# Softmax weights of 26 more attention steps turned on VectorE and through DRAM, with a larger arena and later key jobs

## The chip, the core and the metric

The kernel runs on one core of a Trainium2 chip. Its time is the device time of one execution in microseconds, and the number that counts is the median of several executions. The core's engines are called as the profile calls them: PE (TensorE, matmuls), PEld (its weight loads), DVE (VectorE), ACT (ScalarE), POOL (GpSimd) and SP, whose queue issues nearly all DMAs here. Each engine works through its own instructions in the order in which the program holds them.

## What is computed

Four transformer blocks work one after the other on x of shape 8 x 112 x 256 (8 batches, 112 rows, 256 columns), in float32. All cross attention reads the same context of 8 x 375 x 192. Cut to what matters:

```python
# block 0 and block 1: 16 heads of 64
x = x + attention(ln(x), ln(x)) @ Wo1 + bo1          # self attention
x = x + attention(ln(x), context) @ Wo2 + bo2        # cross attention
a, gate = split(ln(x) @ Wp + bp); x = x + (a * gelu(gate)) @ Wf + bf
# block 2: cross attention alone, 16 heads of 64
x = x + attention(ln(x), context) @ Wo + bo
# block 3: 16 heads of 16, causal and padding masks
x = x + masked_self_attention(ln(x)) @ proj_w + proj_b
x = x + masked_attention(ln(x), context) @ out_w + out_b
x = x + gelu(ln(x) @ mlp1_w + mlp1_b) @ mlp2_w + mlp2_b
# attention: softmax over the keys of q k^T, times v
```

## The kernel before, in words

**Stages and steps.** The code numbers ten stages: 0 self attention, 1 cross attention and 2 feed-forward of block 0; 3, 4 and 5 the same of block 1; 6 the cross attention of block 2; 7 the self attention, 8 the cross attention and 9 the feed-forward of block 3. An attention stage is cut into steps (st, b, g): batch b and a group g of its heads. A cross step of stages 1, 4 and 6 has 4 heads, 4 steps to a batch; a step of stage 7 has 8 heads, 2 steps to a batch. The order of all steps is written out (`order`, `after`, L1271 and on): stage 7's steps are woven into stage 6 and stage 8, two at a time; (7,0) to (7,4) stand between and behind the steps of batches 4 to 7 of stage 6.

**A step** (`add_step`, L963) has these parts. S (`emit_s`) multiplies q by k into PSUM (L1055), 112 rows of queries by 375 or 112 keys, and emits the softmax: for heads of 64 the row maxima on DVE (L1006), the exponentials with their sums on ACT (L1012), the reciprocals on DVE (L1017) and the division on POOL (L1019); for heads of 16 mask and minimum on DVE (L992) and the exponentials on ACT (L1000), half of these in a part E of its own (`emit_late`), while the division comes later, on the product, in parts R and N. The weights of a head are then 112 queries x 375 (or 112) keys, with queries on the partitions. The product with v needs keys on the partitions, so the weights must be transposed. There are two ways:

- *On PE.* Part T (`emit_t`) transposes each head's weights in pieces of 128 keys by a matmul with the identity (L1085) into PSUM, four to a bank, and a copy on ACT or DVE brings each bank of 448 columns to SBUF (`evac`, L354 and L362, or L1092 and L1095 for heads of 16). PV (`emit_pv`, L1118) then multiplies by v.
- *Turned.* q is laid out with each 28 queries in a quarter of 32 partitions (so S gives 128 rows, of which 112 count), POOL clears the gaps (L718) and the padding (L982), and DVE transposes blocks of 32 x 32 (`flip`, L1028, STREAM_TRANSPOSE at L1033, two to a step). The 32 x 32 blocks are then in the wrong quarters: four DMAs write them to a DRAM buffer (`send`, L1039, 192 KB each) and one DMA reads them back in order (`fetch`, L961, 768 KB). PV takes them from there. `w_tile` and `d_tile` are two buffers each, so the fetch of a turned step waits for the PV of the turned step two before it. A turned step's S is emitted up to LEAD = 4 steps ahead of its PV (`lead`, L1546), others 2 steps. `turn_until` (L949) emits the DVE transposes of a step late, normally behind the softmax of the next S.

`TURN` (L1280) chooses: stages 1 and 4 are turned from (0,2) through batch 6, stage 6 from (0,2) through batch 3. That is 66 steps; stages 0, 3, 7, 8 and the second half of stage 6 transpose on PE.

**Planner.** PE's order is written by a planner at build time (`Plan`, L86). Projections, norms and feed-forward are items with a cost, a due step and what they need; the main loop (from L1556) emits S, T and PV of the steps in order and fills in items between them. q, k and v of coming steps lie in one SBUF arena of `ARENA` columns, and an item waits until the arena has room; an item that makes them isn't taken more than `ahead` steps before it is due (L269). Key and value jobs (`add_key_jobs`, `add_value_jobs`) are opened, with their first half emitted, by `open_jobs` (L184, called at L1614).

Of the kernel before, what the change touches and what calls it, by code (L numbers as in the profile page):

```python
# [17 lines left out]
S, DC = 375, 192  # L18
# [10 lines left out]
TURNED = (1, 4, 6)  # L29
# [56 lines left out]
class Plan:  # L86
# [4 lines left out]
    def __init__(self, rings, arena, size):  # L91
# [5 lines left out]
        self.now, self.step, self.ahead = 0.0, 0, 7  # L97
# [207 lines left out]
def kernel(ctx: ExitStack, tc: tile.TileContext, a: dict, out: bass.AP):  # L305
# [3 lines left out]
    ARENA = 9900  # L309
# [123 lines left out]
    cmask = const.tile([T, B, T], BF16, name="cmask")  # L433
    rb = const.tile([T, H, 16], F32, name="rb")
# [118 lines left out]
    def add_masks():  # L553
# [4 lines left out]
        def load():  # L558
            m8 = wpool.tile([T, B * (T + S)], U8, tag="w", name="m8")
            nc.sync.dma_start(m8[:, : B * T], a["mask_BxS_bf0"].rearrange("b t -> (b t)").partition_broadcast(T))  # L560
            nc.sync.dma_start(m8[:, B * T :], a["mask_BxS2_bf0"].rearrange("b s -> (b s)").partition_broadcast(T))
            got[src] = m8

        def self_mask():
            nc.gpsimd.tensor_scalar_mul(cmask.rearrange("p b t -> p (b t)"), got[src][:, : B * T], NEG)
            nc.gpsimd.affine_select(
                cmask, cmask, pattern=[[0, B], [-1, T]], compare_op=ALU.is_ge, fill=NEG, base=0,
                channel_multiplier=1,
            )
# [10 lines left out]
        for b in range(B):  # L580

            def ctx_mask(b=b):
                c = B * T + b * S
                nc.gpsimd.tensor_scalar_mul(got[key][:, b, :], got[src][:, c : c + S], NEG)
# [111 lines left out]
    def add_pair_projection(st, ring, j, w, us, deadline, scale=None):  # L696
# [3 lines left out]
        for u in range(us):  # L700
            key = (ring, st, j, u)

            def fn(u=u, key=key):
# [10 lines left out]
                if ring == "q" and st in TURNED:  # L714
                    kinds = [TURN(st, 2 * j + e, u) for e in range(2)]
# [23 lines left out]
    def add_last_projection(st, ring, j, w, wv, deadline, qb, kb=None):  # L739
# [5 lines left out]
        def fn():  # L745
# [8 lines left out]
            for e, key in enumerate(keys):  # L754
                t = place(key)
                for m in range(2):
                    src = ps[:, m * 2 * T : (m + 1) * 2 * T]
                    if ring == "q":
# [180 lines left out]
    def w_tile(s):  # L939
        return stage[:, (turned[s] % 2) * 1536 : (turned[s] % 2 + 1) * 1536]  # L940

    def d_tile(s):
        at = (2 + turned[s] % 2) * 1536
        return stage[:, at : at + 1536].rearrange("p (i x) -> p i x", i=NQ)

    emptied = [0]
    turns = deque()
# [15 lines left out]
    def add_step(st, b, blocks, dh, nk, qs, ks, qap, kap, vtile, mask, opos, ochunk, last=False, pair=None, turn=False):  # L963
# [9 lines left out]
        heads = [h for blk in blocks for h in blk]  # L973
        cell, late, slot = {}, [], {}

        def softmax(bi, blk, ps):
# [9 lines left out]
            if dh == 16:  # L986
# [3 lines left out]
                for n, h in enumerate(blk):  # L990
# [13 lines left out]
                    late.append(exp)  # L1004
                return pr
# [22 lines left out]
        def flip(bi, blk, whole):  # L1028
            w = whole[:, :]
            src = bass.AP(w.tensor, w.offset, [list(w.ap[0]), [nk, len(blk)], [P, nch], [32, NQ], [1, 32]])  # L1030
            dst = w_tile(s).rearrange("p (j h c t) -> p j h c t", j=NQ, h=4, t=32)
# [4 lines left out]
        def send():  # L1036
            dram = bounce.tile([NQ, 32, NQ, 384], F32, tag="b", name="b")
            for i in range(NQ):
                nc.sync.dma_start(  # L1039
                    dram[:, :, i, :].rearrange("j k x -> k j x"),  # L1040
                    w_tile(s)[32 * i : 32 * i + 32].rearrange("p (j x) -> p j x", j=NQ),
# [60 lines left out]
        def emit_pv():  # L1102
# [3 lines left out]
            if turn:  # L1106
                d = d_tile(s).rearrange("p i (h c t) -> p i h c t", h=4, t=32)
# [545 lines left out]
```

## Time and profile before

| What | Value |
|---|---|
| median of 3 executions | 1614.74 us (1613.98 to 1617.81) |
| the profiled execution | 1610.65 us, of which the span of its instructions is 1608.7 us |
| granted TensorE clock, mean | 0.994 |
| PE transposes of weights, L1085 | 1128 (384 of 112 x 112; 496 and 248 of the pieces of stages 1, 4, 6 and 8) |
| DVE transposes, L1033 | 132, busy 123.9 us |
| sends and fetches | 264 of 192 KB and 66 of 768 KB |
| DMA in all | 143.25 MB, 89 GB/s over the span |

The profile is one execution. Its page gives busy time per engine, the span in 40 slices, and a chain that ended last; further views group instructions by line and shape, list them in order of time (the timeline), sum them by stretch (the windows), and say who waited for whom. In the timeline a row gives start, duration, engine, line, what is written from what, a count when equal instructions were merged, and in brackets the idle time before and what ended it. A matmul of float32 values shows as two records, a transpose as one. Records of PE overlap, since matmuls are pipelined: what one costs PE is the distance between starts, not its duration.

In time, stage 1 lies at about 170 to 440 us, stage 4 at 670 to 945, stage 6 at 1040 to 1380 with its second half and (7,0) to (7,4) from 1190 on, and stage 8 with the rest of stage 7 at 1380 to 1575.

### The profile page before, as it was taken

How to read it: one execution, taken by the hardware profiler on the slowest of the kernel's cores; microseconds unless marked ns; L12 is line 12 of the kernel's file. 1: busy time of each engine (PE TensorE's matmuls, PEld its weight loads, DVE VectorE, ACT ScalarE, POOL GpSimd, SP SyncE). 2: the span in 40 equal slices, each digit the busy share in tenths (PEclk: the TensorE clock that was granted, in tenths of full speed). 3: DMA queues.
4: the chain of work that ended last, by engine and by line, in shares of the span. 5: the costliest groups of instructions: out<-in, count | busy, mean ns of one | idle time of the engine just before them, and what ended most of it. 6: DMA issues, size and time to landing. Idle time of an engine off the chain costs nothing.

```text
span 1608.7 us, 28898 instructions
## 1 busy us (share of the span) xinstructions
PE 1564.2 (97%) x10980; PEld 1069.2 (66%) x10980; DVE 842.4 (52%) x1996; ACT 743.9 (46%) x2396; POOL 538.7 (33%) x667
## 2 busy tenths in 40 slices
PE   9999999999999999998999989999999999999999
PEld 8778656565657878665666555665667666766667
DVE  3554565566522344455656532355555555678762
ACT  3453444434421444543444342134445555787772
POOL 1323344344402313334434330343433237212210
PEclk9999999999999999999999999999999999999999
DMA  6020165676601001035666721125650001000000
GB/s 179 9 70 23 51 190 182 192 211 177 191 30 53 20 5 53 28 101 158 194 196 201 207 68 30 38 56 167 192 163 21 1 1 42 31 2 2 2 1 24
DMA packets 74130, 143.25 MB, mean 89 GB/s; under 512 B 6807, under 2 KB 60695, under 8 KB 73991
## 3 DMA queue, kind: packets, MB, share of 16 engines
q1 hardware_dynamic: 73751, 141.23, 29.4%
q8 instruction: 86, 1.41, 0.4%
q14 instruction: 53, 0.43, 0.1%
q10 hardware_dynamic: 240, 0.17, 0.0%
HBM read 87.79 MB, written 52.82 MB: 87 GB/s over the span
## 4 chain that ended last, share of the span: by engine, by line
PE 77%; DVE 7%; ACT 6%; POOL 4%; DMA 3%; issue 2%; SPq 0%; DVEq 0%; ACTq 0%; POOLq 0%
PE mm L674 12%; PE mm L708 10%; PE s L1055 8%; PE mm L1118 8%; PE mm L815 6%; PE mm L1350 6%; PE mm L849 5%; PE mm L1085 5%; PE mm L824 4%; PE mm L774 4%; PE mm L858 3%; ACT pr L1012 3%; DVE stage L1033 2%; POOL pr L1019 2%; DVE nm L1006 2%
## 5 line engine op out<-in xcount | busy, mean ns | idle before, releaser
L1019 POOL TENSOR_TENSOR pr<-pr,rinv 128x750 f32<-128x750 f32 (+2 forms) x224 | 327.0, 1473 | 425.7 <-DVE rinv L1017 405.7
L1012 ACT ACTIVATE pr<-s,nm 128x375 f32<-128x375 f32 (+2 forms) x640 | 302.1, 489 | 244.2 <-DVE nm L1006 208.4
L1006 DVE TENSOR_REDUCE nm<-s 128x2 f32<-128x750 f32 (+2 forms) x224 | 206.4, 952 | 43.7 <-PE s L1055 41.7
L1055 PE MATMUL s<-arena 64*112 64x112 f32 (+4 forms) x1792 | 215.1, 397 | 6.5 <-ACT pr L1012 6.4
L362 DVE COPY arena<-mm 128x375 f32<-128x375 f32 (+6 forms) x198 | 114.9, 590 | 186.6 <-PE mm L858 74.1
L354 ACT COPY arena<-mm 128x375 f32<-128x375 f32 (+5 forms) x182 | 91.8, 509 | 232.8 <-PE mm L858 104.6
L1118 PEld LDWEIGHTS mm<-stage,arena 128*64 128x64 f32 (+5 forms) x3840 | 161.8, 130 | 42.0 <-issue 16.3
L1118 PE MATMUL mm<-stage,arena 128*64 128x112 f32 (+5 forms) x3840 | 180.4, 263 | 4.0 <-DMA stage<-b 2.9
L1055 PEld LDWEIGHTS s<-arena 64*112 64x112 f32 (+2 forms) x1792 | 116.9, 177 | 86.5 <-issue 29.9
L1085 PEld LDWEIGHTS mm<-ident,pr 112*128 112x128 f32 (+2 forms) x1128 | 124.2, 148 | 45.2 <-issue 19.1
L1085 PE MATMUL mm<-ident,pr 112*128 112x112 f32 (+2 forms) x1128 | 144.8, 264 | 8.7 <-ACT pr L1000 3.4
L1033 DVE STREAM_TRANSPOSE stage<-pr 128x768 f32<-128x768 f32 x132 | 123.9, 961 | 34.9 <-POOL pr L1019 30.2
L1000 ACT ACTIVATE pr<-pr,nm 112x375 f32<-112x375 f32 (+1 forms) x256 | 124.6, 491 | 30.9 <-DVE nm L992 30.9
L1012 ACT ACTIVATION_READ_ACCUMULATOR pr<-s,nm 112x1 f32 (+1 forms) x640 | 132.9, 208 | 0.0
L604 POOL TENSOR_TENSOR rs<-ve,mhalf 128x1 f32<-128x1 f32 x70 | 39.6, 566 | 231.1 <-DVE ve L602 231.0
L1017 DVE RECIPROCAL rinv<-sums 128x2 f32<-128x2 f32 (+2 forms) x224 | 37.9, 169 | 112.9 <-ACT pr L1012 112.1
L849 PE MATMUL mm<-L_xattn_Wv,ctxA 128*128 128x512 f32 (+1 forms) x192 | 91.8, 603 | 3.3 <-ACT arena L352 1.0
L815 PE MATMUL mm<-ctxA,L_xattn_Wk 128*128 128x375 f32 x256 | 91.7, 485 | 3.1 <-ACT arena L354 1.7
L354 ACT COPY stage<-mm 112x448 f32<-112x448 f32 (+2 forms) x103 | 54.4, 534 | 81.0 <-PE mm L1085 80.6
L678 DVE TENSOR_TENSOR x<-mm,x 128x256 f32<-128x256 f32 x70 | 29.6, 422 | 116.6 <-PE mm L674 116.3
L708 PE MATMUL mm<-hT,L_xattn_Wq 128*128 128x224 f32 x384 | 83.3, 361 | 1.6 <-DVE arena L362 1.4
L352 ACT ACTIVATE arena<-mm 128x448 f32<-128x448 f32 (+4 forms) x79 | 38.2, 495 | 92.7 <-PE mm L858 57.4
(135 smaller groups left out, 2303.8 us busy)
## 6 DMA issues: line engine op xcount, KB each, us to landing
b<-stage SPq DMA_DIRECT2D x264, 192.0 KB, 3.6
stage<-b SPq DMA_DIRECT2D x66, 768.0 KB, 5.8
L_xattn_Wo<-in_L_xattn_Wo_dram SPq DMA_DIRECT2D x3, 1024.0 KB, 15.2
L_xattn_w_ff<-in_L_xattn_w_ff_dram SPq DMA_DIRECT2D x3, 1024.0 KB, 7.9
L_xattn_Wv<-in_L_xattn_Wv_dram SPq DMA_DIRECT2D x4, 512.0 KB, 4.0
L_xattn_Wq<-in_L_xattn_Wq_dram SPq DMA_DIRECT2D x2, 1024.0 KB, 4.9
L_xattn_Wp<-in_L_xattn_Wp_dram SPq DMA_DIRECT2D x2, 1024.0 KB, 7.0
L_xattn_wq<-in_L_xattn_wq_dram SPq DMA_DIRECT2D x2, 1024.0 KB, 7.3
```

The source lines that it names most:

```text
L354: nc.scalar.copy(dst, src)
L674: nc.tensor.matmul(ps[:, :D], lhsT=oT[:, c, t * P : (t + 1) * P], rhs=got[wv or w][:, c, :], start=(c == 0), stop=(c == n - 1),)
L708: nc.tensor.matmul(ps[:, i * 2 * T : (i + 1) * 2 * T], lhsT=got[w][:, k, m * P : (m + 1) * P], rhs=hT[:, k, lo:hi], start=(k == 0), stop=( ...
L815: nc.tensor.matmul(ps[:, :S], lhsT=got[wv][:, (2 * u + i) * P : (2 * u + i + 1) * P], rhs=ctxA[:, cols], start=True, stop=False,)
L849: nc.tensor.matmul(ps[: KCH[c][1], :], lhsT=lhs(ctxA, slice(0, KA), c), rhs=got[w][:, hf * 512 : (hf + 1) * 512], start=True, stop=False,)
L1006: nc.vector.tensor_reduce(nm[:, :, :ns], sv, AX.X, ALU.max, negate=True)
L1012: nc.scalar.activation(pr[:, bk, sl, :], sv[:, bk, sl, :], AF.Exp, bias=nm[:, bk, sl : sl + 1], accum_out=sums[:, bk, sl : sl + 1],)
L1019: nc.gpsimd.tensor_tensor(pr, pr, rinv[:, :, :ns].unsqueeze(3).to_broadcast([rows, 2, ns, nk]), ALU.mult)
L1033: nc.vector.transpose(dst, src)
L1055: nc.tensor.matmul(tiles[i][:, n % 2, (n // 2) * nk : (n // 2 + 1) * nk], lhsT=qap(h), rhs=kap(h), start=True, stop=True,)
L1085: nc.tensor.transpose(pt[:kl, m * T : (m + 1) * T], cell[h][:, c * P : c * P + kl], ident[:T, :T])
L1118: nc.tensor.matmul(po[p0 : p0 + dp, blk * T : (blk + 1) * T], lhsT=got[vk][:kl, hv * dp : (hv + 1) * dp], rhs=wt, start=(c == 0 and par(h) ...
```

## The change

`TURNED` takes in stage 7, and `TURN` now turns the whole rest of stage 6 (16 more steps) and (7,0) to (7,4) (10 steps): 92 turned steps in place of 66. For stage 7 this needs new code: a mask of 128 rows laid out by quarters, q written piece by piece into quarters, all exponentials emitted with S (no part E), the transposes of 4 x 112 columns padded to 4 x 128, sends of 4 x 128 KB and a fetch of 512 KB. With stage 7 in `TURNED`, its q, its norms and its transposed inputs also fall due two steps earlier. The arena grows from 9900 to 10700 columns; `ahead` falls from 7 to 6; and jobs are opened when due by i + 2.5 in place of i + 3.5 to i + 5.5. The other edits (stages 0 and 3 in `TURN`, `full` at L1591) take effect only if stages 0 or 3 were turned, which they are not.

```diff
-TURNED = (1, 4, 6)
+TURNED = (1, 4, 6, 7)
-        self.now, self.step, self.ahead = 0.0, 0, 7
+        self.now, self.step, self.ahead = 0.0, 0, 6
-    ARENA = 9900
+    ARENA = 10700
-    cmask = const.tile([T, B, T], BF16, name="cmask")
-    rb = const.tile([T, H, 16], F32, name="rb")
+    cmask = const.tile([P, B, T], BF16, name="cmask")
+    rb = const.tile([P, H, 16], F32, name="rb")
...
+            n = sum(TURN(7, b, 0) for b in range(B))
+            for i in range(NQ):
+                v = cmask[32 * i : 32 * i + 32, :n]
+                nc.gpsimd.affine_select(
+                    v, v, pattern=[[0, n], [-1, T]], compare_op=ALU.is_ge, fill=NEG, base=QR * i, channel_multiplier=1,
+                )
+            v = cmask[:T, n:]
             nc.gpsimd.affine_select(
-                cmask, cmask, pattern=[[0, B], [-1, T]], compare_op=ALU.is_ge, fill=NEG, base=0,
-                channel_multiplier=1,
+                v, v, pattern=[[0, B - n], [-1, T]], compare_op=ALU.is_ge, fill=NEG, base=0, channel_multiplier=1,
             )
...
-                    if ring == "q":
+                    if ring == "q" and st in TURNED:
+                        if m == 0:
+                            nc.gpsimd.memset(t.rearrange("p i (n t) -> p (i n) t", t=32)[:, :, QR:], 0.0)
+                        for bt in range(2):
+                            dst, part = t[:, m, bt * P : (bt + 1) * P], src[:, bt * T : (bt + 1) * T]
+                            if TURN(st, 2 * j + bt, 0):
+                                dst = dst.rearrange("p (n t) -> p n t", t=32)[:, :, :QR]
+                                part = part.rearrange("p (n t) -> p n t", t=QR)
+                            else:
+                                dst = dst[:, :T]
+                            evac(dst, part, T, bcols[:, 8 + e : 9 + e], qcols[:, e, qb + m : qb + m + 1])
+                    elif ring == "q":
...
     def w_tile(s):
-        return stage[:, (turned[s] % 2) * 1536 : (turned[s] % 2 + 1) * 1536]
+        at = (turned[s] % 2) * 1536
+        return stage[:, at : at + NQ * width[s]].rearrange("p (j x) -> p j x", j=NQ)
...
+        width[s] = len(heads) * nch * 32
...
                     late.append(exp)
+                if turn:
+                    while late:
+                        late.pop(0)()
+                    turns.append((s, lambda: flip(bi, blk, whole)))
                 return pr
...
-            dram = bounce.tile([NQ, 32, NQ, 384], F32, tag="b", name="b")
+            dram = bounce.tile([NQ, 32, NQ, 384], F32, tag="b", name="b")[:, :, :, : width[s]]
...
-        if dh == 16:
+        if dh == 16 and not turn:
             plan.add(Item(("E", s), 0, emit_late, deps=[(("S", s), 0)]), False)
...
     def TURN(st, b, g):
-        return st in TURNED and (b, g) > (0, 1) and b < (4 if st == 6 else B - 1)
+        if st not in TURNED:
+            return False
+        return {
+            0: b > 1, 1: (b > 0 or g > 1 or 0 in TURNED) and b < B - 1, 3: b > 0,
+            4: (b > 0 or g > 1 or 3 in TURNED) and b < B - 1,
+            6: (b, g) > (0, 1) and b < (B if 7 in TURNED else 4), 7: b < 5,
+        }[st]
...
-                self_step(7, 16, after[(st, b, g)], 0)
-                self_step(7, 16, after[(st, b, g)], 1)
+                self_step(7, 16, after[(st, b, g)], 0, TURN(7, after[(st, b, g)], 0))
+                self_step(7, 16, after[(st, b, g)], 1, TURN(7, after[(st, b, g)], 1))
...
-                full = 4 if seg < 2 and i < lo + 16 else 2
-                if len(waiting) == full:
+                full = 4 if seg < 2 and i < lo + 16 and not {i, i + 1} & set(turned) else 2
+                if len(waiting) >= full:
...
-            plan.open_jobs(1 if i + 1 >= first_of(8, 0) or i + 2 in woven else 2, i + 1.5 + lead(min(nxt, hi - 1)), seg)
+            plan.open_jobs(1 if i + 1 >= first_of(8, 0) or i + 2 in woven else 2, i + 2.5, seg)
```

## The prediction, made before the changed kernel was run

> **What bounds the kernel now.** I read the page first: busy time by engine, and the chain that ended last.
>
> ```profile
> PE 1564.2 (97%) x10980; PEld 1069.2 (66%) x10980; DVE 842.4 (52%) x1996; ACT 743.9 (46%) x2396; POOL 538.7 (33%) x667
> ...
> PE 77%; DVE 7%; ACT 6%; POOL 4%; DMA 3%; issue 2%; SPq 0%; DVEq 0%; ACTq 0%; POOLq 0%
> ```
>
> PE is busy 97% of the span and holds 77% of the chain. Busy PE is not PE at its peak, so the windows by stage come next: stage 4, which is turned already; the stretch that changes (second half of stage 6 and (7,0) to (7,4)); stage 8 behind it; and 7 us at the end of stage 4's run of turned steps. The columns are length, busy time of PE, PEld, DVE, ACT and POOL with counts, granted PE clock, DMA share, GB/s.
>
> ```profile
> 760.00:910.00 150.00, 149.08 (x964) 91.34 (x963) 91.72 (x158) 68.48 (x202) 65.32 (x90) 1.00 0.65 193
> 1190.00:1380.00 190.00, 187.44 (x1554) 131.66 (x1550) 107.35 (x354) 106.02 (x366) 74.81 (x75) 1.00 0.09 26
> 1390.00:1560.00 170.00, 164.00 (x1834) 111.56 (x1827) 127.91 (x496) 132.72 (x424) 34.00 (x59) 1.00 0.01 2
> 929.50:936.40 6.90, 5.61 (x52) 4.98 (x53) 1.41 (x4) 2.06 (x8) 3.67 (x5) 0.51 0.26 99
> ```
>
> In the stretch that changes PE idles 2.6 of 190 us, DVE and ACT are busy 56% each, and the DMA engines nearly rest. So PE work taken out there shortens the span, as long as the rest keeps up. A transpose on PE is priced by its distance to the next start, from PE's timeline in that stretch:
>
> ```profile
> 1246.50 0.55 PE L1085 MATMUL mm<-ident,pr 112*128 112x112 f32 x4
> 1246.88 3.63 PE L674 MATMUL mm<-L_xattn_Wo,oT 128*128 128x256 f32 x16
> 1250.35 0.96 PE L1085 MATMUL mm<-ident,pr 112*128 112x112 f32 x8
> 1251.15 1.89 PE L849 MATMUL mm<-L_xattn_Wv,ctxA 128*119 128x512 f32 x4
> ...
> 1257.00 1.35 PE L1085 MATMUL mm<-ident,pr 112*128 112x112 f32 x12
> 1258.28 0.79 PE L1055 MATMUL s<-arena 32*112 32x112 f32 x16
> ```
>
> 24 transposes take 0.38 + 0.80 + 1.28 = 2.46 us: 0.1025 us each, although one record lasts some 0.26.
>
> **The change, part by part.**
>
> *Removed from PE.* 16 steps x 4 heads x 3 pieces = 192 transposes, and 10 steps x 8 heads = 80. The built program confirms 1128 to 856, with every other kind of matmul equal in number. 272 x 0.1025 = **-27.9 us**. Ends: 0.095 (the row of four) gives -25.8; the 260 transposes that lie in 1190 to 1380 are busy 31.1 us with their tails, 0.120 each, -32.5. With them go waits of PE on the weights and on their copies: transposes on POOL's division 1.6 us in all, and one value job behind a copy 0.9. I take **-2.5**.
>
> *Added to DVE, off the path.* 32 transposes of 768 columns at 0.961 (their row of groups) and 20 of 512, estimated at 0.961 x 512/768 = 0.64: +43.6 us. Of the copies behind PE's transposes, the built order has DVE lose 20 of stage 6 at 0.616 and 10 of stage 7 at 0.617: -18.5. DVE goes from 107 to 132 of some 160 us, 82%. ACT loses 28 and 10 copies at 0.53: 106 to 86 us, 54%. q of stage 7 in 32 pieces in place of 16 costs ACT and DVE about 4 us together (half of their 0.5 each). POOL gets 52 clearings at 0.106 and some q gaps at 0.158: 7 us where it is 39% busy. Its five mask selects, estimated from one of 896 columns at 1.0, grow to 2.9 us around 1016 us, under the feed-forward of block 1. These cost nothing while DVE keeps below PE. The built order says where it does not: (6,7,0) to (7,4,1) and the first steps of stage 8 stand closer together than before, as PE's fillers between them are used up. By the rows' durations DVE there has about as much work as PE. Uncovered, at worst, are 82% to 100% of some 45 us, 8 us; at best nothing. I take **+2**, near the nearest row: stage 8 before, with DVE and ACT at 75% and 78%, leaves PE idle only 6 of 170 us.
>
> *The added wait, at the end of the new run.* A PV now waits for its fetch, and behind it waits all of PE. How long it takes from a step's DVE transposes to its PV is shown by the last turned step of stage 4, whose transposes end at 921.15 (DVE's, SP's and PE's timelines, one after another):
>
> ```profile
> 919.32 1.83 DVE L1033 STREAM_TRANSPOSE stage<-pr 128x768 f32<-128x768 f32 x2
> ...
> 921.17 2.79 SPq L1039 DMA_DIRECT2D b<-stage  x4
> 924.12 3.84 SPq L961 DMA_DIRECT2D stage<-b  x2
> ...
> 929.85 2.51 PE L1118 MATMUL mm<-stage,arena 128*64 128x112 f32 x24 [0.81 <-DMA stage<-b]
> 933.30 2.51 PE L1118 MATMUL mm<-stage,arena 128*64 128x112 f32 x24 [0.95 <-DMA stage<-b]
> ```
>
> Sends, fetch and landing took 933.30 - 921.15 = 12.2 us, and PE waited twice. In the changed program's order the tightest place is (6,7,3). Between its second DVE transpose and its PV stand on PE only a stage 7 S (0.72 by the row at 1258.28), two stage 7 PVs (0.90), a key job (2.11), two small transposes (0.25) and one PV of 4 heads (2.47/2): 5.2 us. So PE waits 12.2 - 5.2 = **7 us**. The same sum for the steps before it gives 9 to 20 us, short by 3 us at most. That counts inside the 7, since a wait of PE moves all later steps.
>
> A wait that long also costs clock. The last window above has a granted clock of 0.51 from 929.5 to 936.4, after waits of PE of 1.73, 0.81 and 0.95 us; 24 PV records that take 1.24 us at full clock took 2.5. Half of 6.9 us is lost at most: I take **+3**, so +10 for this end. Bounds: 1.1 us, the waits at the end of stage 1's run, where 12.4 us of PE work cover the chain; and 16, if the earlier 3 us add and two such clock windows come.
>
> [...]
>
> *Later jobs, larger arena, stages 1 and 4.* No PE work is added. Between S and PV of the turned steps of stages 1 and 4 stand 24 to 47 us of PE work as before, most changed by under 5. But at the end of stage 1's run the cover from transposes to PV falls from 12.4 to 9.6 us, what stage 4's end has. Stage 4's end costs 0.81 + 0.95 of waits, 1.73 behind a crowded S and up to 3.4 of clock, stage 1's 1.1: **+4**, bounds 0 and 6.
>
> *DMA.* 16 x 1.5 MB + 10 x 1.0 MB, written and read back, lie in 160 us: 215 GB/s more on 26, against 193 at a share of 0.65 in stage 4. It fits; I cost it at nothing, and the third rival says what happens if it does not. The weight load of the last feed-forward now stands in SP's queue ahead of the last fetch, (7,4,1); after a PE wait of 7 us it is late by nothing, without it by some 5, so these two do not add.
>
> **Sum** against the profiled execution: -27.9 - 2.5 + 2 + 10 + 4 = -14.4, from 1610.7 to 1596.3. That execution lies 4.1 below the median of the runs shown; from the median, **1600.3 us**, 0.9% faster.
>
> [...]
>
> **Rivals.**
>
> 1. *Nothing given back.* DVE transposes sit behind nothing slow, the chain takes 10 us as in quiet places, stage 1 is unchanged. For it: the first turned batches of stage 6 show no wait for a fetch. Against: the 5.2 us above. -27.9 - 2.5: 1584.
> 2. *DVE and ACT become the bound* from (6,6,0) through stage 8's first steps: 8 us uncovered there, 16 at the end, 5 in stage 1: -30.4 + 29 = about -1, **1613**. For it: DVE transposes stand ahead of x and copies in DVE's queue; at 726 PE waited 4.35 us for an addition behind two of them that waited for POOL. Against: the planner moves copies to ACT.
> 3. *Slower: the chain through DRAM paces every step.* From the end of its S (905.1) to its PV (933.3) the last step of stage 4 took 28.2 us. PE work between S and PV of the 26 new steps is 18.5 to 37.5 us, 27.8 in the mean. S stands 4 steps ahead, so each us of chain beyond that costs 26/4 = 6.5 us. It takes back all 30 us at a chain of 32.4 us, that is if landing slows by 4 us under 240 GB/s. At 33.5 it is -30 + 37: **1622**. Against: in stage 4 landing took 4 to 6 us at 193 GB/s.
> 4. That the change does nothing is excluded: the built order has the 272 transposes gone.
>
> **How the numbers follow.** This kernel's measurement tells about 0.3% from no change, 4.8 us: faster is below 1609.9, slower above 1619.6. Forecast (1587 to 1609.9): 0.57. Rival 1: 0.18. Rival 2 (1609.9 to 1619.6): 0.15. Rival 3: 0.10. So faster 0.75, same 0.15, slower 0.10. The range leaves out half of rival 1 and nearly all above 1614: 1584 to 1614. Bounds of the terms alone would give -32.5 - 2.5 to -25.8 + 8 + 16 + 6 + 0, that is 1580 to 1619.
>
> **What would show it.** Right: 856 records of PE transposes; 1190 to about 1365 in place of 1380 for the same steps; a PE wait of 4 us or more for a fetch before the PV of (6,7,3), with a clock of half behind it; a second half-clock window near 425; stage 8 as long as before. Wrong: waits for fetches all through the woven steps (rival 3), PE idle on DVE or ACT in the woven steps or in stage 8 (rival 2), or none of the waits (rival 1). A new half-clock window in stages 1 or 4 from the moved jobs would be a cost I left out.

## The result, and the profile after

The changed kernel takes 1628.82 us (median of 4, 1627.28 to 1632.63), the kernel before 1614.45: a ratio of 1.0100, interval 1.0081 to 1.0120. It is **slower by 1%**, where 0.9% faster was forecast, and lies outside the range.

The page of the changed kernel, busy time by engine and the chain that ended last (its profiled execution took 1632.63 us, span 1630.8):

```profile
PE 1559.2 (96%) x10708; PEld 1055.4 (65%) x10708; DVE 850.2 (52%) x1991; ACT 739.6 (45%) x2393; POOL 547.5 (34%) x739
...
PE 79%; DVE 7%; ACT 5%; DMA 3%; POOL 3%; issue 3%; SPq 1%; DVEq 0%; ACTq 0%; POOLq 0%
```

PE has 272 instructions fewer and a span 22 us longer. The totals hide why; the waits of PE do not. First the kernel before, then the changed one, the rows that differ most (who waited, for what: us in all, times, longest):

```profile
PE s L1055 <- ACT pr L1012: 6.4, 9, 1.7
PE mm L815 <- DVE x L678: 4.4, 1, 4.4
...
PE mm L1118 <- DMA stage<-b: 2.9, 4, 0.9
```

```profile
PE s L1078 <- ACT pr L1035: 13.7, 17, 3.5
PE mm L1141 <- DMA stage<-b: 12.8, 4, 5.6
```

PE's waits for a fetch (L1141 is the PV) are still four, but 12.8 us in place of 2.9, and S (L1078) waits twice as long for the exponentials. The granted clock adds to it. The windows of the changed kernel (length, busy PE, PEld, DVE, ACT, POOL, clock, DMA share, GB/s), the 7 us at the end of stage 1's run, the stretch shown before, and its end:

```profile
427.90:434.80 6.90, 4.04 (x44) 4.04 (x46) 1.00 (x3) 2.19 (x8) 3.57 (x3) 0.51 0.45 185
1190.00:1380.00 190.00, 174.29 (x1312) 110.77 (x1308) 125.62 (x369) 99.42 (x359) 84.73 (x141) 0.97 0.72 206
1349.00:1396.00 47.00, 36.62 (x262) 26.73 (x266) 20.96 (x74) 17.42 (x61) 26.72 (x41) 0.82 0.68 213
```

PE idles 16 us of the 190 (2.6 before); of the 47 us from 1349 on it idles 10, at a clock of 0.82. Adding up all distances between starts on PE splits each profiled execution into work at full clock, loss by half clock, and idle time:

| us | before | changed | difference |
|---|---|---|---|
| work, of it transposes of weights | 123.0 | 93.0 | -30.0 |
| work, all else | 1432.5 | 1439.7 | +7.2 (S +5.9) |
| lost by half clock while PE worked | 8.2 | 26.2 | +18.0 |
| idle | 39.6 | 66.5 | +26.9 |

And by place, from the start of one S to that of another (us, profiled executions; the last four columns are experiments below):

| from | before | changed | jobs_only | turn_arena | end_b7 | before_early |
|---|---|---|---|---|---|---|
| start to S(6,0,0) | 1040.7 | 1053.2 | 1049.0 | 1048.3 | 1052.4 | 1033.7 |
| to S(6,4,0) | 154.4 | 141.2 | 152.7 | 146.6 | 140.9 | 154.1 |
| to S(6,7,0) | 129.6 | 126.8 | 137.0 | 133.8 | 137.7 | 129.6 |
| to S(8,0,0) | 57.5 | 74.5 | 55.3 | 70.4 | 54.6 | 59.1 |
| to S(8,7,3) | 174.3 | 182.7 | 181.4 | 177.0 | 184.9 | 174.0 |
| to the end | 52.2 | 52.5 | 52.2 | 52.2 | 52.2 | 52.3 |

In stage 6 (rows 2 to 4), where 30 us of transposes went, the changed kernel is 1 us longer. Outside, where no transpose changed, it is 21 us longer. So there are two questions: what gave back the 30, and what cost the 21.

The end of the new run, on three engines of the changed kernel, PE first:

```profile
1349.58 2.87 PE L1078 MATMUL s<-arena 64*128 64x375 f32 x8 [3.48 <-ACT pr L1035]
1353.62 4.75 PE L1141 MATMUL mm<-stage,arena 128*64 128x112 f32 x48 [1.17 <-DMA stage<-b]
...
1372.70 0.97 PE L1141 MATMUL mm<-stage,arena 112*32 112x112 f32 x32
...
1375.89 0.44 PE L1189 MATMUL mm<-ident,rb 128*128 128x128 f32 x2
1381.95 4.77 PE L1141 MATMUL mm<-stage,arena 128*64 128x112 f32 x48 [5.62 <-DMA stage<-b]
```

```profile
1362.10 0.69 DVE L360 TENSOR_SCALAR arena<-mm 128x512 f32<-128x512 f32 x1 [5.40 <-PE mm L875]
1362.71 1.83 DVE L1056 STREAM_TRANSPOSE stage<-pr 128x768 f32<-128x768 f32 x2
...
1371.85 0.97 DVE L1056 STREAM_TRANSPOSE stage<-pr 128x768 f32<-128x768 f32 x1
```

```profile
1365.65 9.44 SPq L1062 DMA_DIRECT2D b<-stage  x7
1375.25 2.98 SPq L979 DMA_DIRECT2D stage<-b  x2
```

The PVs at 1372.70 are those of (7,3,0) and (7,3,1), the PVs at 1381.95 those of (6,7,2) and (6,7,3). The fetch of (6,7,2) may start when the PV of (7,3,0), two turned steps before it, has emptied its buffer. It is issued at 1375.25, since the last sends stand ahead of it in SP's queue and wait for the second DVE transpose of (6,7,3) (1371.85). From 1372.70 to 1381.95 PE has 3.6 us of work and waits 5.62. DVE itself had waited 5.40 us at 1362 for a value job of PE, with the transposes of (6,7,2) behind that copy.

### The profile page after: what moved, and what is told of

Its sections match the earlier page's. It is cut to its first block, busy times and chain, and to the rows that moved or that the text cites. A ratio compares the mean times of both kernels' runs of the same rounds, so it can differ in the third digit from the quotient of the medians.

```text
span 1630.8 us, 28629 instructions
## 1 busy us (share of the span) xinstructions
PE 1559.2 (96%) x10708; PEld 1055.4 (65%) x10708; DVE 850.2 (52%) x1991; ACT 739.6 (45%) x2393; POOL 547.5 (34%) x739
## 3 DMA queue, kind: packets, MB, share of 16 engines
q8 instruction: 84, 1.38, 0.3%
## 4 chain that ended last, share of the span: by engine, by line
PE 79%; DVE 7%; ACT 5%; DMA 3%; POOL 3%; issue 3%; SPq 1%; DVEq 0%; ACTq 0%; POOLq 0%
PE mm L680 12%; PE mm L714 10%; PE mm L1141 10%; PE s L1078 9%; PE mm L832 6%; PE mm L866 6%; PE mm L1387 6%; PE mm L1108 4%; PE mm L875 4%; PE mm L841 4%; PE mm L791 4%; DMA stage<-b 3%; ACT pr L1035 2%; POOL pr L1042 2%; DVE stage L1056 2%
## 5 line engine op out<-in xcount | busy, mean ns | idle before, releaser
L1078 PE MATMUL s<-arena 64*128 64x375 f32 (+5 forms) x1792 | 222.6, 404 | 18.3 <-ACT pr L1035 13.7
L1141 PEld LDWEIGHTS mm<-stage,arena 128*64 128x64 f32 (+5 forms) x3840 | 168.8, 134 | 52.6 <-issue 24.7
L362 DVE COPY arena<-mm 128x375 f32<-128x375 f32 (+5 forms) x180 | 106.3, 600 | 183.1 <-PE mm L875 74.7
L1141 PE MATMUL mm<-stage,arena 128*64 128x112 f32 (+5 forms) x3840 | 187.6, 269 | 13.8 <-DMA stage<-b 12.8
L1078 PEld LDWEIGHTS s<-arena 64*128 64x128 f32 (+3 forms) x1792 | 118.3, 179 | 107.3 <-ACT pr L1035 30.9
L1056 DVE STREAM_TRANSPOSE stage<-pr 128x768 f32<-128x768 f32 (+1 forms) x184 | 166.2, 930 | 37.7 <-POOL pr L1042 34.8
L1019 ACT ACTIVATE pr<-pr,nm 112x375 f32<-112x375 f32 (+2 forms) x256 | 124.6, 491 | 30.4 <-DVE nm L1011 28.8
L1035 ACT ACTIVATION_READ_ACCUMULATOR pr<-s,nm 128x1 f32 (+1 forms) x640 | 132.8, 208 | 0.0
L1108 PEld LDWEIGHTS mm<-ident,pr 112*128 112x128 f32 (+2 forms) x856 | 96.4, 150 | 35.2 <-issue 16.3
L1108 PE MATMUL mm<-ident,pr 112*128 112x112 f32 (+2 forms) x856 | 111.8, 266 | 6.9 <-ACT pr L1019 3.2
L1001 POOL MEMSET pr<- 128x9 f32 (+1 forms) x184 | 18.9, 107 | 189.6 <-DVE stage L1056 161.8
L680 PE MATMUL mm<-L_xattn_Wo,oT 128*128 128x256 f32 x336 | 79.1, 389 | 0.6 <-DVE hT L358 0.6
```

The lines of the kernel that those rows point to most:

```text
L680: nc.tensor.matmul(ps[:, :D], lhsT=oT[:, c, t * P : (t + 1) * P], rhs=got[wv or w][:, c, :], start=(c == 0), stop=(c == n - 1),)
L1019: return nc.scalar.activation(pr, pr, AF.Exp, bias=nm, scale=-1.0, accum_out=bsums[(st, b)][:, h : h + 1])
L1035: nc.scalar.activation(pr[:, bk, sl, :], sv[:, bk, sl, :], AF.Exp, bias=nm[:, bk, sl : sl + 1], accum_out=sums[:, bk, sl : sl + 1],)
L1056: nc.vector.transpose(dst, src)
L1078: nc.tensor.matmul(tiles[i][:, n % 2, (n // 2) * nk : (n // 2 + 1) * nk], lhsT=qap(h), rhs=kap(h), start=True, stop=True,)
L1108: nc.tensor.transpose(pt[:kl, m * T : (m + 1) * T], cell[h][:, c * P : c * P + kl], ident[:T, :T])
```

## The experiments

Ratios are against the kernel before, measured beside it, with the interval. "Work", "half clock" and "idle" are the sums of the table above, for one profiled execution of each kernel. Executions of one kernel differ by several us, and with them the granted clock: those of the kernel before range from 1606.75 us at a clock of 0.997 to 1618.83 at 0.992. So the ratios decide, and the profiles say where.

**The parts of the change.** jobs_only is the kernel before with

```diff
-self.now, self.step, self.ahead = 0.0, 0, 7
+self.now, self.step, self.ahead = 0.0, 0, 6
-ARENA = 9900
+ARENA = 10700
-plan.open_jobs(..., i + 1.5 + lead(min(nxt, hi - 1)), seg)
+plan.open_jobs(..., i + 2.5, seg)
```

> The kernel before with the three scheduling edits alone (arena 10700, ahead 6, jobs opened when due by i + 2.5); the 66 turned steps stay. Theory A (the loss has two sources: the scheduling edits cost some 12 us in stages 0 to 5, where nothing else was changed, and the end of the new run costs the rest): the first S of stage 6 comes at about 1053 us in place of 1040.6, the whole is 10 to 15 us slower than before, about 1627. Theory B (the turned steps are the whole loss, and the shift in stages 0 to 5 comes from the longer run through the planner): within 3 us of before, about 1614.

1631.44 us, **1.0108** (1.0086 to 1.0129). Without one new turned step it is as slow as the changed kernel; theory A, and more. Work +5.0, half clock +1.3, idle +12.8 us. Stages 0 to 5 are 8.3 us longer, as A said in kind (12 expected), stage 8 another 7.1, and stage 6 between them 3.5.

arena_only is the kernel before with `ARENA = 10700` alone, open_only with `i + 2.5` alone.

> The kernel before with the larger arena alone. With the old job settings and the larger arena (turn_arena) stages 0 to 5 had taken 1048 us in place of 1041. Theory A (in that run the larger arena moved the order of stages 0 to 5): first S of stage 6 at 1048, the whole 5 to 10 us slower than before, 1618 to 1623. Theory B (the arena is harmless, the turned steps bring it): within 3 us of before.

1616.92 us, **1.0033** (1.0020 to 1.0046): 5 us slower, at the lower edge of A. In the profiled execution, which lies 3.5 us under the median, stages 0 to 5 are 2.4 us longer and not the 7 of A.

> The kernel before with the later opening of jobs alone (due by i + 2.5). The three settings together cost 17 us there, the arena alone 5. Theory A (jobs opened later leave PE with less to put between S and PV at the ends of runs and in the woven steps, and the loss is of this edit): 1622 to 1628. Theory B (it is ahead 6 which holds work back): within 4 us of before.

1626.41 us, **1.0079** (1.0050 to 1.0108): theory A. The later opening is most of what the settings cost. `ahead = 6` alone was not run; the three together cost about what these two add up to. Its PE at the end of stage 1's run, behind the same lines of the kernel before:

```profile
425.42 1.38 PE L1118 MATMUL mm<-stage,arena 128*64 128x112 f32 x24 [0.57 <-DMA stage<-b]
427.32 1.38 PE L1118 MATMUL mm<-stage,arena 128*64 128x112 f32 x24 [0.53 <-DMA stage<-b]
```

```profile
427.11 4.75 PE L1118 MATMUL mm<-stage,arena 128*64 128x112 f32 x48 [2.92 <-DMA stage<-b]
```

A wait of 2.92 us in place of 1.10, and 48 records that take 4.75 us at half clock in place of 2 x 1.38. In the kernel before a value job of 2.9 us (L849, L858 at 420.55) stands between S(1,7,0) and S(1,7,1), under the fetch; with the later opening it comes behind these PVs (433.45), and PE has only the two S there. The fetch also lands later, 8.2 us after its issue in place of 6.1. The same wait, 2.6 to 3.5 us, is at the ends of stages 1 and 4 in every profile with the later opening there, whatever is turned (but warm, where matmuls were put into it, and nofetch92, where no PV waits). It is not the only way to such a wait: with the larger arena and the old opening (arena_only) PE waits 3.4 us in two pieces at the end of stage 1. And the second half of stage 8 takes 80.4 us in all profiles with the old opening there, 83.5 to 86.6 in all with the later one.

turn_arena is the changed kernel with `ahead = 7` and the old opening; arena and turned steps stay.

> The changed kernel with ahead 7 and jobs opened by i + 1.5 plus the lead, as before; the 26 new turned steps and the larger arena stay. Theory A: the 12 us of stages 0 to 5 are gone, the wait for a fetch and the clock at half at the end of the new run stay (20 us given back of 30): about 1617. Theory B: as the changed kernel, 1628, as the turned steps are all there.

1632.62 us, **1.0119** (1.0095 to 1.0142). Here theory A falls: the costs do not add. With the old settings the 26 turned steps cost 14 us (1.0119 against 1.0033 of arena_only); with the new ones they cost nothing and bring nothing (1.0100 against 1.0108). Stage 8 comes back (177.0), but the new run waits more: 24 us idle from S(6,4,0) to S(8,0,0), against 18.

s6_only leaves stage 7 out:

```diff
-TURNED = (1, 4, 6, 7)
+TURNED = (1, 4, 6)
-6: (b, g) > (0, 1) and b < (B if 7 in TURNED else 4)
+6: (b, g) > (0, 1) and b < B
```

> The changed kernel with stage 7 transposed on PE as before, all of stage 6 from its third step on turned (82 turned steps, 936 PE transposes). Theory A: PE does the 80 transposes of stage 7 again, +8, but these stand between the PVs at the end of the run and cover part of the chain, and DVE has no stage 7 transposes in the way of an S: the 19.5 us of waits and half clock between (6,7,0) and (8,0,0) fall to about 10; about 1627. Theory B, with its cause in DVE's queue for stage 7's transposes: the waits there go to 3 us, and the time falls to about 1617.

1655.40 us, **1.0256** (1.0231 to 1.0281): far outside both. PE waits 18.4 us for fetches (five times, up to 7.5) and 19.7 for exponentials. By the code (`lead`), a turned step gets a lead of 3 in place of 4 when the step two before it is not turned, and so do the steps (b,2) and (b,3) of batches 4 to 7 here, which stand behind stage 7's; whether this is the cause was not tried.

**Where the run ends.** end_b7 is the changed kernel with `7: b < 3` and `b < 7` for stage 6.

> The changed kernel with the run ended one batch earlier: stage 6 turned through batch 6, stage 7 through batch 2, so batch 7 of stage 6 with its own PE transposes (48) and (7,3), (7,4) with theirs (32) stand behind the last turned step; 936 PE transposes, +8 us of PE. Theory A: the end costs what the end of stage 4 costs (a wait of about 3 us and half clock of about 3) in place of 19.5 us: 8 - 19.5 + 7, about 1624. Theory C (the loss there is not the end but DVE, which stands behind x and value copies all through the woven steps): the waits only move, and it is the changed kernel plus 8, about 1636.

1623.61 us, **1.0059** (1.0040 to 1.0079): theory A (about 1624). From S(6,7,0) to S(8,0,0) it takes 54.6 us in place of 74.5, with idle 6.3 for 14.7 and half clock 1.6 for 7.2. The last PV that waits for a fetch does so for 2.00 us, at 1325; behind it PE has the unturned steps to do. A wait of 4.58 us for a copy of DVE (L1115, at 1365) is most of the idle time left:

```profile
1325.70 0.59 PE L1141 MATMUL mm<-stage,arena 112*32 112x112 f32 x16 [2.00 <-DMA stage<-b]
...
1365.64 0.96 PE L1141 MATMUL mm<-stage,arena 112*32 112x112 f32 x12 [4.58 <-DVE stage L1115]
```

Of the 19.9 us that this stretch gains, 10.9 go back in the stretch before (137.7), mostly as PE work: 80 transposes are on PE again.

**Stages 0 to 5 as before.** split takes the old settings up to stage 6:

```diff
 for seg in range(3):
+    plan.arena, plan.ahead = (9900, 7) if seg < 2 else (ARENA, 6)
-plan.open_jobs(..., i + 2.5, seg)
+plan.open_jobs(..., i + 2.5 if seg == 2 else i + 1.5 + lead(min(nxt, hi - 1)), seg)
```

> The changed kernel, but until the end of stage 5 its planner has the settings of before (9900 of the arena's columns, ahead 7, the old opening of jobs), so that PE's order there is that of before; from stage 6 on as changed. Theory A (stages 0 to 5 lose 8 to 12 us by the new order alone, and this is apart from the turned steps): the first S of stage 6 comes at 1041 in place of 1053 us, and the rest is as in the changed kernel: 1616 to 1620. Theory B (the turned steps themselves slow the whole, or the loss moves to another place): 1625 or more.

1624.25 us, **1.0084** (1.0063 to 1.0104). S(6,0,0) is at 1044.5 us, and the rest takes 577.7 us as in the changed kernel (577.6). PE's order up to stage 6 is that of the kernel before, which took 1040.7; the 3.8 us between them are half clock and idle time, in two executions of the same order. The time lies between A and B, and against the changed kernel (1.0100) the gain isn't clear of noise: the intervals overlap. The profiled execution is 8.6 us shorter, but that of the changed kernel was its slowest.

> As the run before, and the new run of turned steps ended one batch earlier (stage 6 through batch 6, stage 7 through batch 2). Theory A: both gains add, 1623.6 - 8 to 12, so 1612 to 1616, level with the kernel before. Theory B: 1620 or more.

1615.83 us, **1.0028** (1.0011 to 1.0045): the two add within the intervals, as A said. Against end_b7 (1.0059) the old settings up to stage 6 bring some 5 us. split3_b7 has in addition, from two steps ahead of stage 8 on, `plan.ahead = 7` and the old opening:

> As the split kernel with the run ended one batch earlier, and in addition from the steps ahead of stage 8 on the planner has ahead 7 and the old opening of jobs again. Theory A (the new job settings cost some 6 us in stage 8, as stage 8 was 6 to 10 us longer in every run with them, 2.7 in the one without them): stage 8's steps take 174 to 177 us in place of 180, the whole 1609 to 1612, level with before or better. Theory B (stage 8 is longer as work moved there from stage 6): no gain, 1616.

1616.81 us, **1.0009** (0.9996 to 1.0022), level with the kernel before. Its stage 8 takes 180.3 us, 80.4 in the second half as A said, but 99.9 in the first, with 5.7 us more work than before: B is right there. So with most of the other costs taken out (the larger arena, `ahead = 6` and the later opening stay in stage 6), 192 transposes fewer are worth nothing: work -15.4 us, idle +13.4, half clock +6.6.

**The half clock.** warm puts 43 idle matmuls into the long waits of the changed kernel:

```diff
+WARM = {(1, 6, 8): 9, (4, 6, 8): 8, (6, 7, 8): 16}   # first head of the step, before its PV
+if (st, b, heads[0]) in WARM: warm(WARM[(st, b, heads[0])])
+if (st, b, heads[0]) == (6, 7, 12): warm(10)   # before its S
```

> The changed kernel with 43 idle matmuls (identity by identity, 128 x 128, nothing reads them) put where PE waits long: 9 ahead of the PV of (1,6,2), 8 ahead of that of (4,6,2), 10 ahead of the S of (6,7,3), 16 ahead of the PV of (6,7,2). All other instructions keep their order. They take some 0.3 us each and fit into the waits of 3.2, 2.9, 3.5 and 5.6 us. Theory A (a wait costs twice: itself, and the half clock behind it): the granted clock stays at 1.00 behind these places, and 8 to 13 us come back, 1616 to 1621. Theory B (the half clock falls into time in which PE would have waited anyway): no gain or a little loss, 1627 to 1631.

1627.28 us, **1.0104** (1.0085 to 1.0123): theory B. The windows of warm at the places shown as 0.5 before:

```profile
427.90:434.80 6.90, 5.96 (x66) 4.39 (x68) 1.95 (x4) 0.85 (x3) 2.31 (x2) 1.00 0.18 75
1380.00:1387.00 7.00, 6.57 (x69) 5.76 (x66) 0.42 (x1) 1.55 (x3) 0.81 (x3) 1.00 0.76 253
```

The clock is back (loss 12.8 us in place of 26.2), the time is not. Waits and dummies together stand where waits and half clock stood: PE waits 7 us less and does 13 us more. That leaves 7 us between these two executions; 5.5 of them are that the changed kernel's lies 3.8 us over its median and warm's 1.7 under. The dummies were longer than the time they filled, so the price of the clock alone stays open; it is no gain that can be had this way.

**DVE, the softmax buffers and the trip.** a9932 is the changed kernel with `ARENA = 9932`, a9932_pr5 has in addition `name="ppool", bufs=5`.

> The changed kernel with an arena of 9932 columns in place of 10700 (about the least with which it can be built; with 9900 there is no room for a key of stage 7). It is the control for the next run, and tells what the arena does beside the turned steps. Theory A (the arena's size only shuffles the order): within 8 us of the changed kernel, 1620 to 1636, with the same two great waits at the end of the new run. Theory B (the larger arena itself is the cost): stages 0 to 5 as before, first S of stage 6 at 1041, and 1615 to 1619.

1622.06 us, **1.0059** (1.0037 to 1.0081): theory A, with the two great waits still there (3.48 us for exponentials, 5.29 for a fetch). But it is 0.4% faster than the changed kernel, about what the arena cost alone (arena_only), and S(6,0,0) is at 1045.6 in place of 1053.2, so B has a part.

> As the run before with five buffers for the weights in softmax (pr) in place of four; PE's order is the same. In the changed kernel an S waited 3.5 us at 1349 for the exponentials, these for a pr buffer, and the buffer for a DVE transpose that stood behind an addition to x. Theory A (PE is held up by DVE through the pr buffers in the woven steps): the waits of S on ACT's exponentials between 1190 and 1400 us fall from some 6 us to under 2, and the time is 4 to 8 us under the run before. Theory B (the chain through DRAM sets the pace there, and an earlier S only waits later for its fetch): within 2 us of the run before.

1624.42 us, **1.0067** (1.0041 to 1.0092), no difference: theory B. PE of a9932, then of a9932_pr5:

```profile
1340.25 0.90 PE L1078 MATMUL s<-arena 64*128 64x375 f32 x4 [3.48 <-ACT pr L1035]
...
1344.29 1.95 PE L1141 MATMUL mm<-stage,arena 128*64 128x112 f32 x18 [1.31 <-DMA stage<-b]
```

```profile
1344.33 0.99 PE L1078 MATMUL s<-arena 64*128 64x375 f32 x4 [3.35 <-ACT pr L1035]
1348.41 1.95 PE L1141 MATMUL mm<-stage,arena 128*64 128x112 f32 x18 [3.09 <-DMA stage<-b]
```

With a fifth buffer the first half of S comes without a wait, but the second waits as long as the first did, and the wait for the fetch behind it grows from 1.31 to 3.09 us. The exponentials (ACT) still wait for a DVE transpose to empty a buffer, now one buffer later:

```profile
1343.05 0.57 ACT L1035 ACTIVATE pr<-s,nm 128x375 f32<-128x375 f32 x1 [3.07 <-DVE stage L1056]
```

So one buffer more moves the wait and doesn't remove it.

nofetch26, nofetch92 and before_nofetch66 let PV read a constant in place of the fetched weights, so that these products are left out:

```diff
 wt = d[:kl, :, slot[h], c, 0:QR] if turn else cell.pop((h, c))
+if turn and (st == 7 or st == 6 and b > 3):   # nofetch92, before_nofetch66: if turn
+    wt = ctxA[:kl, :P].rearrange("p (i t) -> p i t", t=32)[:, :, :QR]
```

> The changed kernel, but the PVs of the 26 new turned steps read a constant block of the same shape (128 x 4 x 28 of the context) in place of the fetched weights, so they do not wait for the trip through DRAM; DVE transposes, sends and fetches all stay, as does PE's order. Left out is the true product of these steps. Theory A (the trip through DRAM at the end of the new run is the cost): the waits for a fetch at 1353 and 1382 go, and with them the S that waits behind them and the half clock; (6,7,0) to (8,0,0) takes some 58 us in place of 74.5, the whole 1611 to 1616. Theory B (DVE and ACT, and not the trip, hold PE there): the waits move to S on ACT's exponentials and to copies; 1622 or more.

> The same for all 92 turned steps. Theory A: in addition the waits of 3.2 and 2.9 us at the ends of stages 1 and 4 and the half clock behind them go, 6 to 9 us: 1603 to 1609. Theory B (what PE does not wait for there it waits for right behind): as the run before, within 3 us.

> The kernel before with the same edit for its 66 turned steps: what the trip through DRAM costs it. Its waits for a fetch are 1.1 us at the end of stage 1 and 1.8 at that of stage 4, with 3.4 of half clock. Theory A: 3 to 6 us faster, 1608 to 1611. Theory B: no change.

1663.32, 1695.07 and 1624.61 us, **1.0311**, **1.0509** and **1.0076** (intervals within 0.0028 of these). All are slower than the kernels they come from. Only B of nofetch26 ("1622 or more") leaves room for that, and the waits of S for exponentials are its own; none gave a reason. PE's order is the same, but only PE's is written by hand (L320): those of the other engines are set when the kernel is built, from what needs what. With nothing waiting for the transposes, they come later: the mean time from the end of S to the second DVE transpose of the new steps rises from 15.0 (stage 6) and 13.8 us (stage 7) to 20. PE's waits in nofetch26:

```profile
PE s L1078 <- ACT pr L1035: 21.7, 22, 3.5
PE s L1078 <- DVE nm L1011: 12.7, 11, 3.4
PE mm L1143 <- DMA stage<-b: 5.9, 2, 3.0
```

The two fetch waits left are those of stages 1 and 4. S waits 34.4 us for exponentials and maxima, against 15.5 in the changed kernel. So the runs don't tell the price of the trip: they took the wait away and changed the orders of DVE, ACT and POOL at the same time. That the later transposes make S wait is likely, but not shown apart from the rest.

flip_early moves them the other way, right behind the softmax of their own step:

```diff
-turn_until(s)
+turn_until(s + (st == 7 or st == 6 and b > 3))
```

> The changed kernel, but the DVE transposes of the 26 new turned steps are emitted right behind the softmax of their own step, not behind that of the next S; PE's order is the same, DVE's is not. In the changed kernel it took 12 to 22 us from the end of S to the second DVE transpose in the woven steps, and 15 to 28 in nofetch26, which lost 35 us. Theory A (it is DVE's lateness with these transposes that makes the trip through DRAM late at the end of the run and holds the pr buffers): that time falls under 10 us, the waits at 1349, 1353 and 1382 fall from 10.3 to under 4 us, the whole to 1615 to 1621. Theory B (earlier transposes wait in DVE's queue for POOL's division, and copies and maxima that PE needs stand behind them): new waits of PE on DVE of 2 to 4 us each, as the 4.35 us at 730 in the kernel before; 1628 or more. Theory C (the fetch must wait for the PV two steps before, whatever DVE does): the wait of 5.6 us stays within 1.5, 1624 to 1628.

1636.47 us, **1.0146** (1.0113 to 1.0180). The transposes come 4 us earlier (11.1 and 10.1 us), S waits less for exponentials (9.0 for 13.7 us), and PE waits *more* for fetches, 21.1 us in twelve waits:

```profile
PE mm L1141 <- DMA stage<-b: 21.1, 12, 5.0
PE s L1078 <- ACT pr L1035: 9.0, 16, 1.7
```

B's time, but C's wait (4.96 us for 5.62), and neither mechanism whole. SP's queue in it:

```profile
1261.52 9.90 SPq L1062 DMA_DIRECT2D b<-stage  x8
1271.52 0.92 SPq L979 DMA_DIRECT2D stage<-b  x2
```

The fetch of (6,5,0) at 1271.52 had its data in DRAM at 1257.6 and its buffer free with the PVs of (6,4,2) and (6,4,3), which began at 1263.5. But the sends of two later steps are now issued ahead of it, and the second of these waits for DVE until 1269.6. In the changed kernel this fetch was issued at 1263.5, 2.4 us after its data had landed.

> The best version so far (level with before: ratio 1.0009) with the earlier DVE transposes in stages 6 (from batch 4) and 7. Theory A: 4 to 8 us faster than it, so under the kernel before by 0.2 to 0.4%. Theory B: slower than it. Theory C: within 2 us of it.

1617.28 us, **1.0028** (1.0010 to 1.0046): theory C by the medians, 1 to 3 us slower than split3_b7 (1.0009) with intervals that overlap. In the kernel before, the same edit is `turn_until(s + 1)`:

> The kernel before with the earlier DVE transposes in all its 66 turned steps; stages 1, 4 and 6 leave DVE 55 to 60% busy there. Theory A: the waits at the ends of stages 1 and 4 shrink, 2 to 6 us faster. Theory B: waits of PE on DVE behind POOL's division, at places such as 730, 5 us slower or more.

**1603.30 us, 0.9939** (0.9924 to 0.9955): theory A in kind, but 10 us where A had 2 to 6: 0.6% **faster than the kernel before** and 1.6% faster than the changed one. PE's order is that of the kernel before, instruction for instruction by line. At the end of stage 1's run there is no wait left:

```profile
425.99 1.43 PE L1055 MATMUL s<-arena 64*112 64x375 f32 x8
427.34 2.53 PE L1118 MATMUL mm<-stage,arena 128*64 128x112 f32 x48
```

The second DVE transpose ends 9.9 us after S in stage 1 (15.4 before) and 9.2 in stage 4 (13.2), no PV waits for a fetch there, and the wait of 4.35 us for x at 730 falls to 2.23. Stages 0 to 5 are 7.0 us shorter. The profiled executions differ by 6 us, most of it idle time; the rest of the 10 us is that the profiled execution of the kernel before lies some 3 us under its median and this one 1.8 over.

## Why the prediction was wrong

Two terms of the sum were too small, the settings (+4) and the end of the new run (+10), and the sum took them to be independent, which they are not.

**Removed from PE: right.** 272 transposes went, and their line does 30.0 us less at full clock (forecast 27.9). Not foreseen: all other matmuls together take 7.2 us more, S alone 5.9, as longer distances between starts that no view shows as a wait. S takes 4.0 us more in jobs_only too, where no further step is turned, so most of this goes with the settings.

**Later jobs, larger arena: the step that failed.** It was costed at +4, bounds 0 and 6, with the words that no PE work is added and that the cover at the end of stage 1 falls from 12.4 to 9.6 us. jobs_only measures it at +17, open_only at +13. The place named was right (the waits at the ends of stages 1 and 4), the size there too small, and two places were left out: stage 8 (+7.1 in jobs_only) and stage 6 (+3.5 as a whole, +7.4 in batches 4 to 6 alone), where the order changes although nothing more is turned. Nor does PE's work stay the same: no matmul is added, but it takes 5.0 us more at full clock. The size holds for the settings alone: put back to the old opening and `ahead = 7`, the changed kernel gets no faster (turn_arena).

**The end of the new run: right mechanism, wrong wait, too small.** It was +10, bounds 1 and 16, from a chain of 12.2 us less 5.2 of cover at (6,7,3). Measured are 12.3 us more idle and 7.2 more half clock between S(6,7,0) and S(8,0,0), less 2.5 of work: +17. The sum followed one step's own chain from its transposes to its PV. What ended last was the fetch of the step before, (6,7,2): it waits for the PV two turned steps back and for the sends ahead of it in SP's queue, so that the time from PV pair to PV pair counts (9.25 us, with 3.6 of work), not the chain of one step. That rule was in the description of the kernel and not in the sum. And the earlier steps, "short by 3 us at most" and counted inside, had waits of their own, 3.48 and 1.17 at 1350. That it is the end of the run that costs this is shown by end_b7; whether the trip or DVE's order sets it is open, since the nofetch runs moved both.

**DVE and ACT crowding: above +2, inside the bounds of 0 to 8.** Waits of S on exponentials rose by 7.3 us, 5.4 of them between 1190 and 1400, where there were none; idle time from S(6,4,0) to S(6,7,0) rose by 3.5. So the sign named for rival 2 came in part, but a fifth buffer for the weights changes nothing (a9932_pr5).

**Half clock.** Forecast +3 at the new end and up to 3.4 at that of stage 1; found 7.2 at the new end and 18 in all. Warm took 13 us of it away and gained nothing, with as much work put in; so how much of the half clock would cost time by itself is not shown.

**DMA: right as a rate, not as a queue.** 206 GB/s at a share of 0.72 in the stretch, and fetches land in 5.7 us in the median as before (5.8). (The added traffic is 35.7 MB, over the 160 us of the forecast 223 GB/s and not 215.) What holds a fetch back at the end is when it is issued (that of (6,7,2) at 1375.25): behind the PV that empties its buffer (begun at 1372.70) and behind the sends ahead of it in SP's queue (until 1375.09).

**Terms that do not add.** -30 for the transposes and +17 for the settings would make -13; measured is +16. So with the new settings the turned steps give back all 30 us, not the 12 of the forecast, and with the old ones 14 more. How the error divides between the two terms therefore depends on which is counted first. Rival 3 had the sign right at a chance of 0.10, but not the mechanism: from the end of S to the landing of its fetch it is some 28 us in the mean of the new steps, not 32, and PE waits for a fetch four times, 12.8 us in all. Of the signals named, the 856 records, the wait for a fetch before the last PVs of stage 6 with half clock behind it, and the window near 425 came. "1190 to about 1365" did not (from S(6,4,0) to S(8,0,0) it takes 201 us where it took 187), nor did "stage 8 as long as before" (+8.4).

The profiled execution of before lies 3.8 us under the median of this comparison, that of the changed kernel 3.8 over. So the spans differ by 22 us, the medians by 14.4; the tables by place say where, not how much to the microsecond.

## What to carry over

A parameter of a planner (how far ahead, how large an arena, when a job opens) is a change of its own: run it alone before pricing anything beside it, and then with the rest, as the two need not add. Here the settings cost as much alone as the whole slowdown (+17 us where +4 was forecast), and the opening and `ahead`, taken out of the changed kernel, gave nothing back. For work that goes through a ring of buffers and a queue, find the last steps of the run and count from the release of the buffer and from what stands ahead in the issuing queue (here the fetch of (6,7,2) was issued 2.55 us after the PV that empties its buffer had begun, and PE waited 5.62 us for it); one step's own chain is only a lower bound. And look for slack at the producer first: the same trip through DRAM, started 4 to 5.5 us earlier in the stages that have room for it, made the kernel 0.6% faster, where 26 more turned steps made it 1% slower.

## What the runs showed of the hardware

In the profiles of the kernel before and of the changed one the granted clock is full or half, and all windows of half clock begin on one grid of 3.41 us and last one, two or three steps of it (3.41, 6.83 or 10.24 us), but for the one at the end of the kernel. In the kernel before, the windows at 728, 930, 1022 and 1104 follow grid steps in which PE was idle for 2.14, 1.64, 2.02 and 1.68 us by its records; a step with 1.57 (1363) was not followed by one. In the changed kernel, from 60 us on, half clock came behind the steps at 220, 425, 937, 1032, 1107, 1346, 1377, 1408 and 1510, with PE idle for 2.09, 1.64, 1.64, 2.40, 1.77, 3.38, 3.41, 2.06 and 1.21 us, and not behind those at 1029, 1271 and 1452, with 1.97, 1.65 and 1.64. So no single idle time separates the steps that half clock followed from the others in these records.

In flip_early a fetch that was ready stood behind sends in SP's queue: that of (6,5,0) had its data in DRAM at 1257.6, and the PVs that free its buffer began at 1263.5, but it was issued at 1271.52, right behind eight sends that took from 1261.52 to 1271.42.
